# A second queue for row fetches: ScalarE takes over one gathered token of 26 tiles

## The chip, the core and the metric

The kernel runs on one core of a Trainium2 chip. The metric is device time in microseconds (us), from the kernel's start to its end. Engines are named as the profile names them: PE is TensorE (matmul), PEld its weight loads, DVE is VectorE, ACT is ScalarE, POOL is GpSimd, SP is SyncE. A name with a q (SPq) is an engine's queue, which issues transfers.

## The reference

A recommendation model for a batch of 16384 rows, in float32:

```
tok  = word_emb[token_idx].mean(axis=1)        # 32 tokens a row, table 50000 x 300
e1   = emb_mh1[mh1_idx].mean(axis=1)           # 20 indices a row, table 1000 x 64
e2, e3 likewise                                # tables 5000 x 64 and 10000 x 64
o1..o4 = emb_oh*[oh*_idx]                      # one index a row, small tables
emb  = concatenate([tok, e1, e2, e3, o1, o2, o3, o4], axis=1)     # 748 columns
wide = the sum of a scalar looked up for every small index
h    = relu(emb @ W1 + b1); h = relu(h @ W2 + b2); h = relu(h @ W3 + b3)   # 1024, 512, 256
out  = sigmoid(h @ Wd + bd + wide)
```

## The kernel before

The batch is cut into 128 tiles of 128 rows; a row of the batch is a partition. A tile goes through 11 steps, and the program's main loop runs over steps (1435 of them). One order for each engine is written out by hand: what the loop emits first stands first in each engine's queue, and an engine works its queue in order. Steps of different tiles overlap: counts of one tile, sums of the one before it, layers of earlier ones.

**Small tables.** They are not gathered. DVE makes one-hot rows by comparing an iota with the indices (`one_hots`, L402, tile `hot`), ACT scales a part of them (L409), PE multiplies them into counts (`counts`, L420, tile `pc`), ACT packs these into `cnt` (L423), and PE multiplies the counts of a whole tile with the tables kept on the chip (`small_sums`, L455, tile `pg`), which DVE adds up (L445). There are two buffers for `hot` and two for `pc`. The three layers run on PE at L578, and ACT evicts them at L589 into `h`.

**Tokens.** The 32 token rows of a tile are fetched from the 50000-row table in memory. POOL does most: one indirect DMA fetches the row of one token position for all 128 partitions, 1200 bytes each (L303, into `tok_rows`). Two positions make a group, a tile has 16 groups, and six buffers of two gathers each stand between POOL and DVE, which adds each gather onto the sum `own` (`add_up`: L279 for the first group, L281 and L286 after it). The adds follow the gathers by three groups (`TOK_LAG`) and are paced over the steps, so they stand in DVE's queue between the one-hots. The last add of a tile writes the features `g`.

**Rows by SyncE.** For two of three tiles (those from tile 4 with `t % 3` not 0, 83 in all) the last token position, 31, is not gathered. SP fetches it row by row (`fetch`, L347, into `fetched`): SP loads the position's 128 indices as a row (`load_column`, L320), DVE turns them into byte offsets with two small operations (`column_offsets`, L329 and L330), SP loads 32 of them at a time into registers (L338) and issues one transfer of 1200 bytes for each row. A fetch starts 25 or 19.5 steps ahead of the step by which the tile is summed, and its 128 rows are spread over 16.5 steps. Each transfer of a hardware queue takes the next of eight semaphores in turn, and waits until the transfer that had it before has landed.

SP also loads indices (`load_indices`, L357 and L361), weights and tables, and stores results (L631).

Of the kernel before, what the change touches and what calls it, by code (L numbers as in the profile page):

```python
# [31 lines left out]
COLUMN_AHEAD = 4  # L32
COLUMN_LAG = 1
LOADS = 32
ROW_BYTES = 4 * TOK_D
WAKE = 27
EARLY = 3
# [40 lines left out]
def kernel(  # L78
# [39 lines left out]
    ohp = ctx.enter_context(tc.tile_pool(name="onehot", bufs=HOT_BUFS))  # L118
    cp = ctx.enter_context(tc.tile_pool(name="counts", bufs=2))
    fp = ctx.enter_context(tc.tile_pool(name="fetched", bufs=2))  # L120
    gp = ctx.enter_context(tc.tile_pool(name="g", bufs=3))
    wp = ctx.enter_context(tc.tile_pool(name="wide", bufs=2))
    xp = ctx.enter_context(tc.tile_pool(name="x", bufs=1))
# [18 lines left out]
    chunk_at = [1, 1 + 2 * ROW, 1 + 4 * ROW, WIDE_AT, G_COLS - 2 * P, G_COLS - P]  # L142
    NK = len(chunk_rows)
    N_EARLY = 3

    ident = const.tile([P, P], F32, name="ident")
    make_identity(nc, ident)
# [22 lines left out]
    nc.vector.tensor_copy(own[:, 0 : n_h // 2], iota_s.bitcast(F32))  # L170
    iota = own[:, 0 : n_h // 2].bitcast(BF16)

    first = const.tile([P, 2, N_SMALL], I32, name="first")
    lookups = [("e1", N_MH), ("e2", N_MH), ("e3", N_MH), ("o1", 1), ("o2", 1), ("o3", 1), ("o4", 1)]
    at = 0
    for f, n in lookups:
# [1 line left out]
        at += n  # L178

    terms = const.tile([P, n_h, 3 * ROW], BF16, name="terms")  # L180
    minus_count = const.tile([P, P], BF16, name="minus_count")
    nc.vector.tensor_single_scalar(minus_count, ident, -1.0 / COUNT, op=ALU.mult)

    zeros = const.tile([P, ROW], F32, name="zeros")
    nc.vector.memset(zeros, 0.0)

    def load_tables(part0, tag):
        raw = hp.tile([P, PART, ROW], F32, name="raw", tag=tag)
        for f in SMALL:
            table, (h0, h1) = tables[f], slices[f]  # L190
            full, rest = divmod(table.shape[0], P)
            a, b = max(h0, part0), min(h0 + full, part0 + PART)
            if a < b:
                nc.sync.dma_start(
                    out=raw[:, a - part0 : b - part0, :],
                    in_=table[(a - h0) * P : (b - h0) * P, :].rearrange("(h p) d -> p h d", p=P),
                )
            if rest and part0 <= h0 + full < part0 + PART:
                nc.sync.dma_start(out=raw[rest:P, h0 + full - part0, :], in_=zeros[rest:P, :])
                nc.sync.dma_start(out=raw[0:rest, h0 + full - part0, :], in_=table[full * P :, :])  # L200
        return raw

    def convert_tables():
# [48 lines left out]
    def load_weights():  # L252

        nc.vector.memset(w1_sb[0:1, 3, :], 0.0)
        for k, rows in enumerate(chunk_rows):
            for at, a, b in rows:
                nc.sync.dma_start(out=w1_sb[at : at + b - a, k, :], in_=w1[a:b, :])
        nc.sync.dma_start(out=w2_sb, in_=w2.rearrange("(k p) m -> p k m", p=P))
        nc.sync.dma_start(out=w3_sb, in_=w3.rearrange("(k p) m -> p k m", p=P))
        for sb, dram in ((wd_sb, wd), (b1_sb, b1), (b2_sb, b2), (b3_sb, b3), (bd_sb, bd)):  # L260
            nc.sync.dma_start(out=sb, in_=dram)

    g_of = {}

    def features(t):
        if t not in g_of:
            g_of[t] = gp.tile([P, G_COLS], F32, name="g")
        return g_of[t]

    n_groups = N_TOK // TOK_GROUP  # L270
    n_all = B // P * n_groups + TOK_LAG
    summed = set()
# [15 lines left out]
    def tokens():  # L288

        under_way = []  # L290
        for n in range(n_all):
            if n < n_all - TOK_LAG:
                t, q = divmod(n, n_groups)
                it = token_indices[t // NSUB][:, t % NSUB, :].bitcast(U32)
                tok_rows = tokp.tile([P, TOK_GROUP * TOK_D], F32, name="tok_rows")
                rows = []
                for r in range(TOK_GROUP):
                    j = q * TOK_GROUP + r
                    if j == N_TOK - 1 and t in fetched:
                        rows.append(fetched.pop(t))  # L300
                        continue
                    rows.append(tok_rows[:, r * TOK_D : (r + 1) * TOK_D])
                    nc.gpsimd.indirect_dma_start(  # L303
                        out=rows[-1],
                        out_offset=None,
                        in_=word,
                        in_offset=bass.IndirectOffsetOnAxis(ap=it[:, j : j + 1], axis=0),
                    )
                under_way.append((t, q, rows))
            if n >= TOK_LAG:  # L310
                add_up(*under_way.pop(0))
            yield 1

    fetched, columns = {}, {}
    word_bytes = word.bitcast(U8).rearrange("n d -> (n d)").unsqueeze(0)

    def load_column(t):

        columns[t] = fp.tile([1, P], I32, name="column")
        nc.sync.dma_start(  # L320
            out=columns[t], in_=idx[t * P : (t + 1) * P, N_TOK - 1 : N_TOK].rearrange("n o -> o n")
        )

    def column_offsets(t):


        column = columns[t]
        low = ROW_BYTES & -ROW_BYTES
        nc.vector.tensor_single_scalar(column, column, ROW_BYTES // low, op=ALU.mult)  # L329
        nc.vector.tensor_single_scalar(column, column, low.bit_length() - 1, op=ALU.logical_shift_left)  # L330

    def fetch(t):


        rows = fp.tile([P, TOK_D], F32, name="fetched").bitcast(U8)
        column = columns.pop(t)
        for p0 in range(0, P, LOADS):
            _, values = nc.values_load_multi_w_load_instructions(  # L338
                column[:, p0 : p0 + LOADS],
                engines=[mybir.EngineType.SP],  # L340
                min_val=0,
                max_val=(word.shape[0] - 1) * ROW_BYTES,
                skip_runtime_bounds_check_because="the indices are rows of the table",
            )
            for i, value in enumerate(values):
                p = p0 + i
                nc.sync.dma_start(out=rows[p : p + 1, :], in_=word_bytes[:, bass.ds(value, ROW_BYTES)])  # L347
                if p == P - 1:
                    fetched[t] = rows.bitcast(F32)
                yield 1  # L350

    def load_indices(blk):


        b0 = blk * BLOCK
        it = idxp.tile([P, NSUB, N_TOK], I32, name="it")
        nc.sync.dma_start(  # L357
            out=it, in_=idx[b0 : b0 + BLOCK, 0:N_TOK].rearrange("(s p) c -> p s c", p=P)
        )
        ix = keyp.tile([P, 2, N_SMALL], I32, name="ix")  # L360
        nc.sync.dma_start(  # L361
            out=ix, in_=idx[b0 : b0 + BLOCK, IDX_MH:IDX_COLS].rearrange("(p f) c -> p f c", f=2)
        )
        token_indices[blk] = it
        return ix

    def lookup_keys(ix):
# [4 lines left out]
        keys = keyp.tile([P, 2, 2 * N_SMALL], BF16, name="keys", tag="keys")  # L372
        view = keys.rearrange("p w (f c) -> p w f c", f=2)
        nc.vector.tensor_copy(view[:, 0], low)
        nc.vector.tensor_add(view[:, 1], ix, first)
        return keys

    def key_columns(keys):
# [215 lines left out]
    def mlp(block, part=None):  # L594
# [19 lines left out]
        def finish():  # L614
# [13 lines left out]
            b0 = block.first * P  # L628

            def store():  # L630
                nc.sync.dma_start(out=out[b0 : b0 + n, :].rearrange("(a b) o -> o a b", b=P), in_=y)  # L631

            stores.append([STORE_LAG, store])

# [67 lines left out]
    fetches = [(summed_at(t) - FETCH_AHEAD[t % 3], t) for t in range(FETCH_FROM, tiles) if t % 3]  # L702
    fetching = []

    def speed(step):

        left = n_steps - step
        return 1 / (TILE_STEPS if left > WAKE else TILE_STEPS_SUMS if left > STEPS + EARLY else TILE_STEPS_LAST)
# [11 lines left out]
            block_of.update({t + k: block for k in range(n)})  # L720
        return block_of[t]

    ctx.enter_context(tc.manual_schedule())
    ix = load_indices(0)
    toks = Paced(tokens())
    tables_on_chip = convert_tables()
# [6 lines left out]
    for step in range(n_steps):  # L733
# [10 lines left out]
        if t < tiles:  # L744
# [5 lines left out]
            if i < STEPS - 1:  # L750
                hot = one_hots(sc, s, i + 1)
            elif t + 1 < tiles:
                hot = one_hots(next_sc if s == NSUB - 1 else sc, (s + 1) % NSUB, 0)
            flush_outputs()
            counts(cnt, hot_now, i)
            tables_on_chip.to(TABLE_PACE * (step - 2))
            if t == 1 and i == STEPS - 1:
                load_weights()
        else:
            flush_outputs()  # L760
        if sums:
            run_sums(sums, early_sums.get(i, 0), step, step)
        outputs = list(rows_out)
# [8 lines left out]
                    completed = step  # L772
        if complete and layers is None and step > completed:
            layers, target = start(complete.pop(0)), 0
        for at, t_f in fetches:
            if step == int(at) - COLUMN_AHEAD:
                load_column(t_f)
            if step == int(at) - COLUMN_LAG:
                column_offsets(t_f)
            if step == int(at):  # L780
                fetching.append((at, Paced(fetch(t_f))))
        for at, rows in list(fetching):
            rows.to(P * (step + 1 - at) / FETCH_STEPS)
            if step + 1 - at >= FETCH_STEPS:
                rows.finish()
                fetching.remove((at, rows))
        toks.to(tokens_by(step + 1))
        if t < tiles and more and s == 1 and i == (5 if t > 1 else 9):
            next_sc, evict = key_columns(next_keys)
# [26 lines left out]
    while complete or layers:  # L816
        if layers:
            layers.finish()
        layers = Paced(mlp(complete.pop(0))) if complete else None
    for _, k, ks in waiting:  # L820
        block = block_for(k)
        block.transpose(k, ks)()
# [43 lines left out]
```

## Time and profile before

| | |
|---|---|
| median of 3 runs | 5055.15 us (5052.5 to 5058.55) |
| the profiled execution, its time | 5052.86 us |
| its span, first to last instruction | 5050.9 us |
| granted TensorE clock, mean | 0.992 |
| busy: PE, DVE, ACT, POOL | 4810.5, 3716.8, 2723.9, 3798.2 us |
| gathers of POOL | 4013 |
| rows fetched by SP | 10624 = 83 x 128 |
| DMA engines' mean busy share | 4 to 5 tenths after the start |

A row of the groups reads: line, engine, operation, tile written and tiles read, count; then busy time in us and mean ns of one; then the idle time of the engine before these instructions, and what ended most of it. A row of the waits reads: who waited, for what, us in total, how often, the longest. A row of the timeline reads: start, duration, engine, line, and in brackets the idle time before it. A row of one source line gives least, median and greatest duration in ns. A row of the windows gives the stretch, then for PE, PEld, DVE, ACT and POOL the busy us and the number of instructions, then the granted clock, the DMA share and GB/s.

### The profile page before, as it was taken

Reading aid. Unit: us, or ns where it says so; the run is one execution under the profiler, and the core shown is the slowest. Engines: PE = TensorE matmul, PEld = TensorE weight load, DVE = VectorE, ACT = ScalarE, POOL = GpSimd, SP = SyncE. Lnnn points to the kernel's source line nnn. Section 1 sums busy time; section 2 is a strip of 40 time slices with the busy share of each in tenths; the row PEclk is TensorE's granted clock in tenths of the full one; section 3 lists DMA queues with packets and bytes.
Section 4 is the critical chain, followed back from the end, with each engine's and each line's share of the span. In section 5 each row is a group of like instructions: output and inputs, shape, how many; then the busy total and the mean of one; then the engine's idle time right before and its main releaser. Section 6 shows DMA issues by size and latency. Waiting matters only on the chain.

```text
span 5050.9 us, 117299 instructions
## 1 busy us (share of the span) xinstructions
PE 4810.5 (95%) x36356; PEld 3711.0 (73%) x36356; DVE 3716.8 (74%) x6778; ACT 2723.9 (54%) x3658; POOL 3798.2 (75%) x4020
## 2 busy tenths in 40 slices
PE   6799999999999999999999999999999999999999
PEld 4677776776777677677677777667767888888898
DVE  6777777777777777777777777777777777777774
ACT  5555555555555555555555555555555555555552
POOL 7777777777777777777777777777777777777775
PEclk9899999999999999999999999999999999999999
DMA  7444444444444444444444444444444444444443
GB/s 203 127 129 129 128 128 128 128 129 128 128 128 129 128 129 128 129 129 128 129 128 128 129 129 128 128 128 128 129 129 128 129 129 128 129 128 129 129 127 100
DMA packets 282526, 653.64 MB, mean 129 GB/s; under 512 B 140443, under 2 KB 151707, under 8 KB 281895
## 3 DMA queue, kind: packets, MB, share of 16 engines
q0 software_dynamic: 192624, 616.65, 45.3%
q1 hardware_dynamic: 89271, 29.49, 2.8%
q8 instruction: 284, 4.65, 0.4%
q14 instruction: 347, 2.84, 0.2%
HBM read 645.64 MB, written 0.07 MB: 128 GB/s over the span
## 4 chain that ended last, share of the span: by engine, by line
DMA 34%; DVE 19%; PE 17%; issue 16%; POOL 11%; ACT 2%; SPq 0%; DVEq 0%; POOLq 0%; ACTq 0%
DMA tok_rows<-in_word_emb_dram,it 34%; POOL tok_rows L303 11%; PE ph L578 8%; DVE hot L402 7%; DVE own L286 6%; PE pg L455 6%; DVE own L281 3%; PE pc L420 2%; DVE g L445 1%; ACT hot L409 1%; DVE own L279 0%; ACT cnt L423 0%; PE pc L496 0%; PE po L620 0%; SPq L347 0%
## 5 line engine op out<-in xcount | busy, mean ns | idle before, releaser
L303 POOL DMA_INDIRECT tok_rows<-in_word_emb_dram,it x4013 | 3797.3, 946 | 1225.2 <-issue 709.0
L409 ACT ACTIVATE hot<-hot 64x768 bf16<-64x768 bf16 (+1 forms) x1408 | 1155.4, 821 | 2065.3 <-DVE hot L402 2053.6
L455 PE MATMUL pg<-terms,cnt 128*128 128x195 bf16 x17664 | 1720.8, 249 | 57.2 <-DVE g L445 56.7
L455 PEld LDWEIGHTS <-cnt 128*128 128x128 fp8e3 x17664 | 1527.9, 98 | 105.7 <-issue 77.0
L578 PE MATMUL ph<-x,w_sb 128*128 128x384 f32 (+5 forms) x4932 | 1474.5, 436 | 21.1 <-ACT h L589 14.9
L402 DVE TENSOR_TENSOR hot<-own,sc 128x1656 bf16<-128x1656 bf16 (+1 forms) x1408 | 1394.1, 990 | 104.1 <-PE pc L420 12.5
L286 DVE TENSOR_TENSOR own<-own,tok_rows 128x300 f32<-128x300 f32 x1792 | 857.4, 478 | 593.9 <-DMA tok_rows<-in_word_emb_dram,it 551.5
L578 PE MATMUL ph<-h,w_sb 128*128 128x384 f32 (+2 forms) x4160 | 1225.6, 434 | 14.7 <-ACT h L589 14.6
L423 ACT ACTIVATE cnt<-pc 128x828 uint16<-128x828 f32 (+1 forms) x1408 | 1186.2, 842 | 68.8 <-PE pc L420 47.7
L281 DVE TENSOR_TENSOR own<-own,tok_rows 128x300 f32<-128x300 f32 x1920 | 917.7, 478 | 380.9 <-DMA tok_rows<-in_word_emb_dram,it 330.9
L578 PEld LDWEIGHTS ph<-x,w_sb 128*128 128x128 f32 (+1 forms) x4932 | 829.3, 191 | 313.9 <-ACT h L589 27.5
L420 PEld LDWEIGHTS <-hot 128*128 128x128 bf16 x8192 | 589.3, 98 | 531.1 <-issue 216.4
L578 PEld LDWEIGHTS ph<-h,w_sb 128*128 128x128 f32 x4160 | 698.8, 191 | 268.4 <-ACT h L589 29.7
L420 PE MATMUL pc<-hot 128*128 128x138 bf16 x8192 | 732.9, 224 | 109.6 <-ACT hot L409 81.0
L589 ACT ACTIVATE h<-ph,b_sb 128x384 f32<-128x384 f32 (+2 forms) x723 | 378.6, 524 | 123.9 <-PE ph L578 108.6
L445 DVE TENSOR_REDUCE g<-pg 128x130 f32<-128x390 f32 (+1 forms) x512 | 258.6, 505 | 68.4 <-PE pg L455 66.6
L500 DVE TENSOR_TENSOR x<-pc,scale 128x768 f32<-128x768 f32 x127 | 120.7, 950 | 43.8 <-PE pc L496 43.6
L496 PE MATMUL pc<-ident,g 128*128 128x128 f32 x762 | 107.0, 277 | 9.2 <-ACT cnt L423 7.9
L279 DVE TENSOR_TENSOR own<-tok_rows 128x300 f32<-128x300 f32 x128 | 61.4, 480 | 70.0 <-DMA tok_rows<-in_word_emb_dram,it 67.6
L496 PEld LDWEIGHTS pc<-ident,g 128*128 128x128 f32 x762 | 83.2, 142 | 14.7 <-ACT cnt L423 13.1
L620 PE MATMUL po<-h,wd_sb 128*1 128x384 f32 (+2 forms) x208 | 66.0, 438 | 2.0 <-ACT h L589 2.0
L627 ACT ACTIVATE x<-po,bd_sb 1x384 f32<-1x384 f32 (+2 forms) x52 | 26.7, 514 | 54.3 <-PE po L620 54.1
(57 smaller groups left out, 471.5 us busy)
## 6 DMA issues: line engine op xcount, KB each, us to landing
fetched<-in_word_emb_dram SPq DMA_DIRECT2D x10624, 1.2 KB
tok_rows<-in_word_emb_dram,it POOLq DMA_INDIRECT x4013
ix<-in_idx_dram SPq DMA_DIRECT2D x64, 64.0 KB
w_sb<-in_W_dram SPq DMA_DIRECT2D x6, 512.0 KB
raw<-in_mh_dram SPq DMA_DIRECT2D x4, 682.5 KB
it<-in_idx_dram SPq DMA_DIRECT2D x64, 32.0 KB
w_sb<-in_W_dram SPq DMA_DIRECT2D x1, 2048.0 KB
column<-in_idx_dram SPq DMA_DIRECT2D x83, 0.5 KB
```

Of the source, the lines that this page charges most:

```text
L281: nc.vector.tensor_add(tok_sum, tok_sum, a)
L286: nc.vector.tensor_add(to, tok_sum, b)
L303: nc.gpsimd.indirect_dma_start(out=rows[-1], out_offset=None, in_=word, in_offset=bass.IndirectOffsetOnAxis(ap=it[:, j : j + 1], axis=0),)
L402: nc.vector.tensor_tensor(hot[:, 0 : 2 * rows, :].rearrange("p i (n d) -> p i n d", d=2), iota.rearrange("p (n d) -> p n d", d=2).unsqueez ...
L409: nc.scalar.activation(upper, upper, AF.Copy, scale=UPPER)
L420: nc.tensor.matmul(pc[:, k // n, at : at + n_h], hot[:, 2 * k, 0:P], hot[:, 2 * k + 1, :], start=True, stop=True)
L423: nc.scalar.activation(cnt[:, :, b : b + rows].rearrange("l h (g k) -> l h g k", g=2), pc[:, :, 0 : n * n_h].rearrange("l g (k h) -> l h g ...
L445: nc.vector.tensor_reduce(field_columns(features(t), pair), pg[:, 0:n, :].rearrange("p f (c d) -> p f d c", c=3), AX.X, ALU.add,)
L455: nc.tensor.matmul(pg[:, j, :], by_slice[:, h, :], terms[:, h, :], start=(h == h0), stop=(h == h1 - 1))
L496: nc.tensor.transpose(pt[:, j // n, j % n, :], g[:, c : c + P], ident)
L578: nc.tensor.matmul(to, weights[: src.shape[0], k, m * P : (m + 1) * P], src, start=(k == 0), stop=(k == len(srcs) - 1),)
L589: nc.scalar.activation(dst()[:, m, 0:n], ph[:, 0:n], AF.Relu, bias=bias[:, m : m + 1])
```

## The change

Token position 30 of 26 tiles (from about tile 12 on) is no longer gathered by POOL. ACT fetches it row by row, with a queue of its own, into new buffers `fetched_scalar`: it loads the column of indices, DVE makes offsets of it, ACT loads 8 offsets at a time into registers and issues a transfer for each row. A helper `sync_dma` stands ahead of each of SP's transfers: when the next of the eight semaphores would be the seventh or eighth (`SCALAR_LANES`), ACT issues first, so that two rows of ACT follow six transfers of SP. A column for ACT is chosen when half the rows of the one before are out; the tile chosen is the first that is summed late enough at 2.55 rows a step and 5 steps of margin.

Rows of SP are now emitted in two portions in each step, before and after `counts`, where they were emitted in one portion later in the step. In `add_up` a row that is fetched comes first in its group. Two constants move into one of the new buffers, the columns share one tile, `first` is half as large, and POOL's order is kept by tokens in place of the written-out order.

The diff, cut to its core:

```diff
+LANES = 8
+SCALAR_LANES = (6, 7)
+SCALAR_FROM = 12
+SCALAR_RATE = 2.55
+SCALAR_MARGIN = 5.0
+SCALAR_LOADS = 8
+SCALAR_WANTED, SCALAR_LEAST = 8, 2
...
+    fa = ctx.enter_context(tc.tile_pool(name="fetched_scalar", bufs=2))
...
+    def hardware_dma(queue, **operands):
+        dma = queue.dma_start(**operands)
+        if transfers and transfers[-1][0] is not queue:
+            tc.add_manual_dep(
...
+        transfers.append((queue, dma.ins.name))
+
+    def sync_dma(**operands):
+        while len(transfers) % LANES in SCALAR_LANES and scalar_row and scalar_row[0]():
+            pass
+        hardware_dma(nc.sync, **operands)
...
-                    if j == N_TOK - 1 and t in fetched:
-                        rows.append(fetched.pop(t))
+                    if (t, j) in fetched:
+                        rows.insert(0, fetched.pop((t, j)))
                         continue
...
+        def choose(self, rows_before):
+            least = self.step + (rows_before + P) / SCALAR_RATE + SCALAR_MARGIN
+            t = next((t for t in range(tiles_all) if self.summed_at(t) >= least), None)
...
+        def load(self, free):
+            if len(self.values) >= (SCALAR_WANTED if free else SCALAR_LEAST):
+                return
...
+            self.values += load_offsets(self.column, self.loaded, SCALAR_LOADS, mybir.EngineType.Activation)
+            self.loaded += SCALAR_LOADS
+
+        def __call__(self):
...
+            value = self.values.pop(0)
+            p = self.row
+            hardware_dma(nc.scalar, out=self.rows[p : p + 1, :], in_=word_bytes[:, bass.ds(value, ROW_BYTES)])
+            self.row += 1
...
+    def fetch_rows(step, part):
...
+        for at, rows in list(fetching):
+            rows.to(P * (step + part - at) / FETCH_STEPS)
...
+        if scalar_row:
+            scalar.load(scalar.issued == issued)
...
+            fetch_rows(step, 0.5)
             flush_outputs()
             counts(cnt, hot_now, i)
+            fetch_rows(step, 1)
...
-        for at, rows in list(fetching):
-            rows.to(P * (step + 1 - at) / FETCH_STEPS)
```

## The prediction

> **What bounds the kernel now.** I read the page's busy table first, then the costliest groups, then the waits, then the timeline.
>
> ```profile
> PE 4810.5 (95%) x36356; PEld 3711.0 (73%) x36356; DVE 3716.8 (74%) x6778; ACT 2723.9 (54%) x3658; POOL 3798.2 (75%) x4020
> L303 POOL DMA_INDIRECT tok_rows<-in_word_emb_dram,it x4013 | 3797.3, 946 | 1225.2 <-issue 709.0
> ```
>
> The shares point at TensorE (PE) and would have us pass over POOL, but the POOL row must be read with its idle time: (3797.3 + 1225.2) / 4013 = 1.2515 us for each gather, and 4013 of them are 5022.5 us of a span of 5050.9. The timeline of POOL shows a metronome:
>
> ```profile
> 2000.12 0.94 POOL L303 DMA_INDIRECT tok_rows<-in_word_emb_dram,it  x1 [0.30 <-issue]
> 2001.37 0.94 POOL L303 DMA_INDIRECT tok_rows<-in_word_emb_dram,it  x1 [0.30 <-issue]
> 2002.62 0.95 POOL L303 DMA_INDIRECT tok_rows<-in_word_emb_dram,it  x1 [0.31 <-issue]
> ```
>
> Every gap is 0.30 us, whatever releaser is named beside it. From the records of all gathers, only 16 of 4012 start more than 1.3 us after the one before, 3 us of excess in all. So POOL never waits for a buffer: VectorE (DVE) always frees one in time, and it is DVE that waits for gathers.
>
> ```profile
> DVE own L286 <- DMA tok_rows<-in_word_emb_dram,it: 551.5, 853, 3.1
> DVE own L281 <- DMA tok_rows<-in_word_emb_dram,it: 330.9, 455, 2.9
> DVE hot L402 <- PE pc L420: 12.5, 19, 1.4
> ACT hot L409 <- DVE hot L402: 2053.6, 1272, 5.4
> ```
>
> DVE waits some 900 us for gathers and 12.5 us for PE's buffers; ACT (ScalarE) waits 2053.6 us for DVE. POOL sets the time; PE is close behind it.
>
> **The change, part by part.**
>
> *26 gathers leave POOL.* The changed order has 26 fewer gathers and nothing in their place: 26 x 1.2515 = 32.5 us. This lies wholly on the path.
>
> *Fetched rows are added first.* At the end of the last tile one add now runs before the last gather lands, where two follow it today:
>
> ```profile
> 5025.98 0.48 DVE L281 TENSOR_TENSOR own<-own,tok_rows 128x300 f32<-128x300 f32 x1 [0.72 <-DMA tok_rows<-in_word_emb_dram,it]
> 5026.49 0.47 DVE L286 TENSOR_TENSOR g<-own,fetched 128x300 f32<-128x300 f32 x1
> ```
>
> That saves 0.5 us. Elsewhere the adds keep their number and places. DVE gets 26 x (0.204 + 0.215) = 11 us of column arithmetic (durations of the same two operations at L329 and L330), beneath its 900 us of waiting.
>
> *ScalarE's queue.* In the changed order ACT's activations stand exactly as before. Between them come 3328 row transfers, 26 column loads and 416 register loads of 8 values. For a row the nearest rows are SyncE's (SP's):
>
> ```profile
> L347 SPq MOVE fetched<-in_word_emb_dram x10624: 29/29/39, 114.9 to 4996.0; - x197
> L347 SPq DMA_DIRECT2D fetched<-in_word_emb_dram x10624: 217/225/395, 115.0 to 4996.0; - x197
> L338 SPq TENSOR_LOAD <-column x332: 2026/2127/2360, 112.8 to 4983.6; - x166
> ```
>
> Undisturbed, SP starts a row every 0.32 us (the median of the starts). So ACT's sequencer gets 3354 x 0.32 = 1073 us. A load of 32 values takes 2.13 us; 8 values take between 0.53 (in proportion) and 2.13 us. The Trainium skill speaks against the lower end: "DMA: Bandwidth & Descriptors", section "Latency and other measured facts", gives such a load a floor of about 0.6 us. A line from 0.6 at one value to 2.13 at 32 gives an estimate of 0.94 for 8. By proportion the 416 loads are 220 us, by the page's floor 391, at the most 886. I take 391.
>
> Is it hidden? ACT's own work is 2723.9 us. Over the 1276 steps from tile 12 on (a step is 3.48 us between two `counts`) the addition is 1.15 us a step, against 1.46 of waiting for `hot` (2053.6 / 1408). It hides better than that, because ACT's sequencer runs ahead of its engine: its semaphore event for L627 at 770.500 lies inside the activation of 770.49 to 771.33. A pair of rows placed behind `hot` (0.84 us) or `cnt` (0.84) can thus be issued while that one runs.
>
> What doesn't hide is the wait on the two semaphores: a pair waits until the pair before has landed. In the trace's semaphore records a row of SP's lands 1.79 us after its start (median; 1.43 and 2.10 at the 5th and 95th per cent). A bad step: `hot` at 0, pair behind it, `cnt` at 0.84, second pair held to 1.8 and done at 2.5; the next `hot` is due at 3.5. With a load the sequencer is free at 3.4. So it fits, barely, and what stands behind it when it doesn't is `hot`, and PE behind `hot`: by the records PE starts `counts` 0.95 us (median; 0.35 at the lower quartile) after `hot` ends. Laying the changed ACT order over the trace's own ready times, `hot` comes about 0.05 us later on average. I put it at 0 to 5 us, and take 1.
>
> *SyncE's queue.* SP keeps its rows, with six semaphores for eight. Six rows take 6 x 0.32 = 1.92 us; 25% of rows land later than that, by 0.032 us averaged over all rows. A fetch of 128 rows thus loses between 0 and 4.1 us; since a delayed row also delays those behind it, not all adds up, and I take 3. Moving the rows to two places of a step changes only the order on SP, which has no engine waiting but DVE. SP has room:
>
> ```profile
> SPq L338 <- DVE own L281: 179.6, 27, 10.3
> SPq L338 <- DVE own L286: 161.0, 25, 11.1
> SPq L338 <- DVE hot L402: 119.1, 15, 12.5
> ```
>
> With the four smaller rows of this kind SP waits 577.8 us before its 83 fetches, 7.0 us each, and by the records the last row lands at least 10.8 us before DVE adds it. A step 0.65% shorter takes 0.4 of the 7.0, the semaphores 3: 3.6 us remain, cost nothing.
>
> *Two queues at once.* No row of this trace has two engines issuing. The Trainium skill, "Perfetto Trace Analysis", section "DMA Instruction — HWDGE (DVE, Sync)", says that the block that generates descriptors is shared and locked for one issuer: that speaks against the change. By the rule at its worst each ACT row holds SP up for a whole issue, 0.225 us; at the least for the generation alone: the 128-element column load (557 ns at L320) against a row's 225 gives 2.6 ns for each element, so nearly nothing for one row. I take the low end, some 0.03 us, since that slope is the nearest measurement; 40 ACT rows to a fetch (3328 / 83) then cost 1.2 of the 3.6 us. By the other end see below.
>
> *PE.* It must do the same work in 32 us less.
>
> ```profile
> 3500.00:4500.00 1000.00, 972.35 (x7570) 802.75 (x7569) 751.73 (x1360) 551.80 (x748) 756.31 (x800) 1.00 0.48 128
> 4900.00:5000.00 100.00, 97.52 (x947) 94.82 (x947) 56.61 (x112) 34.78 (x70) 75.36 (x80) 1.00 0.47 126
> ```
>
> Between 500 and 4900 us PE idles 146 us (4400 less the busy time of those windows). About 28 of the 33 us fall there: it must go from 96.7 to 97.3% busy; the two stretches above are at 97.2 and 97.5. As part of its idle time is DVE held by gathers, I count 1 us lost.
>
> **Sum.** 5050.9 - 32.5 - 0.5 + 1 + 1 = 5019.9 us of span; the profiled execution took 5052.86, 2 us over its span, so 5021.9; the median of the runs is 2.3 above that execution: 5024 us, 0.6% less. A measurement of this kernel can tell about 0.2%, 10 us, from no change.
>
> **The rivals.**
>
> *SyncE falls behind (slower).* The lock above is real. SP's spare 6.6 us a fetch then goes to 40 ACT rows; once rows are spread out, the six semaphores cost only some 1.4 us a fetch, so the turn comes at (6.6 - 1.4) / 40 = 0.13 us for each ACT row. Past it every fetch ends later than the one before, and after the 10.8 us margin DVE stands at the add of the last group, with `hot` queued behind it and PE behind that. At 0.225 us: 40 x 0.225 + 0.8 - 6.6 = 3.2 a fetch, over 77 fetches 246, less 10.8 and the 33 gained: about +200, 5255 us. At 0.15: about +35, 5090. For it: SP's issue occupies 70% of its time. Against: the slope above. Chance 0.12, with the neighbouring case that ACT does not issue beneath an activation (then 1.15 us a step meet 1.46 of waiting, half of it in the wrong place; 50 to 150 us of PE stalls by the same overlay, 5070 to 5170), which the event at 770.500 speaks against: 0.10. Together 0.22 slower.
>
> *PE becomes the bound.* If half or more of its idle time is its own (waits for its own results: L445 to L455 and back show 67 and 57 us), the gain is cut to a third to two thirds: 5033 to 5045. For: 97% busy. Against: DVE's 900 us. Chance 0.10, of which 0.04 within 0.2%.
>
> *Nothing to measure.* The POOL time is won and handed to stalls of ACT or SP of the same size: 5045 to 5065, chance 0.06. That the gathers are not taken out is excluded by the order.
>
> *My forecast*, 5016 to 5033: chance 0.62. With the faster part of the PE case 0.68 faster, 0.10 the same, 0.22 slower. The range from 5016 reaches into the slower cases to 5085, so that about 0.16 lies above it and 0.04 below. The forecast's own range is 5016 to 5033.
>
> **What would show it.** Right: 3987 gathers still 1.25 us apart with no gap; PE's idle time down by about 30 us; ACT's wait for `hot` down, PE's wait for `hot` (81 us at L420) not up by more than 10; SP's wait before its loads down from 578 to about 200 to 350 us; an ACT row near 0.23 us, a load near 0.9. Wrong: POOL gaps over 1.3 us released by DVE, DVE waiting for `fetched`, SP rows over 0.37 us apart, or gathers no longer evenly spaced.

## The result, and the profile after

The changed kernel takes 5020.66 us (median; 5019.4 to 5021.1 over 4 runs), the kernel before 5054.3 in the same comparison: the ratio is 0.9932 with a 95% interval of 0.9915 to 0.9949, some 34 us or 0.7% faster. The profiled execution took 5021.06 us, with a span of 5019.3. Nine of the twelve experiments below were run on three chips on which the kernel before itself takes 7220 to 7240 us; each is compared with that. The other three, which come first, ran where it takes 5057 to 5058 us.

First the busy table of the changed kernel's page, the shares of the chain of work that ended last, and the row of gathers:

```profile
PE 4806.3 (96%) x36356; PEld 3721.3 (74%) x36356; DVE 3748.7 (75%) x6830; ACT 2726.5 (54%) x3658; POOL 3774.2 (75%) x3994
...
PE 37%; DMA 26%; DVE 15%; issue 12%; POOL 9%; ACT 1%; SPq 1%; ACTq 0%; DVEq 0%; POOLq 0%
...
L337 POOL DMA_INDIRECT tok_rows<-in_word_emb_dram,it x3987 | 3773.3, 946 | 1219.3 <-issue 754.1
```

(3773.3 + 1219.3) / 3987 = 1.2522 us for each gather, the pitch of before, and 26 fewer of them. POOL's timeline shows the same beat:

```profile
2001.83 0.95 POOL L337 DMA_INDIRECT tok_rows<-in_word_emb_dram,it  x1 [0.30 <-issue]
2003.08 0.95 POOL L337 DMA_INDIRECT tok_rows<-in_word_emb_dram,it  x1 [0.30 <-issue]
2004.33 0.94 POOL L337 DMA_INDIRECT tok_rows<-in_word_emb_dram,it  x1 [0.30 <-DVE own L319]
```

Then the waits (who, for what, us in total, times, longest):

```profile
ACT hot L508 <- DVE hot L501: 1664.0, 1089, 5.0
...
DVE own L319 <- DMA tok_rows<-in_word_emb_dram,it: 468.5, 683, 2.8
...
DVE own L314 <- DMA tok_rows<-in_word_emb_dram,it: 221.0, 333, 3.1
...
ACT hot L508 <- DMA fetched_scalar<-in_word_emb_dram: 95.1, 92, 3.0
...
ACT h L688 <- DMA fetched_scalar<-in_word_emb_dram: 62.9, 84, 1.7
...
PE pc L519 <- ACT hot L508: 51.7, 34, 4.0
...
ACT cnt L522 <- DMA fetched_scalar<-in_word_emb_dram: 49.8, 67, 1.6
...
DVE hot L501 <- PE pc L519: 37.7, 55, 2.1
```

DVE still waits some 690 us for gathers, 190 less than before. New are 208 us in which an activation of ACT stands behind a row that waits for the landing of an earlier one. They do not lengthen PE's wait for `hot`, which fell from 81 to 52 us. DVE waits for no row that SP fetched. Next come the rows of the two hardware queues, where one line now issues for both (least, median, greatest ns):

```profile
L161 SPq DMA_DIRECT2D fetched<-in_word_emb_dram x10624: 217/225/604, 114.3 to 4966.2; - x197
...
L161 ACTq DMA_DIRECT2D fetched_scalar<-in_word_emb_dram x3328: 213/214/746, 309.9 to 4790.8; - x196
```

```profile
L375 ACTq TENSOR_LOAD <-columns x416: 716/763/1013, 307.0 to 4770.6; - x139
```

Where ACT's rows went is best seen in its timeline:

```profile
2000.23 0.84 ACT L508 ACTIVATE hot<-hot 64x768 bf16<-64x768 bf16 x1 [2.19 <-DVE hot L501]
2000.31 0.77 ACTq L161 DMA_DIRECT2D fetched_scalar<-in_word_emb_dram  x2
2001.13 0.87 ACT L522 ACTIVATE cnt<-pc 128x828 uint16<-128x828 f32 x1
2002.23 0.77 ACTq L161 DMA_DIRECT2D fetched_scalar<-in_word_emb_dram  x2
2003.05 0.84 ACT L508 ACTIVATE hot<-hot 64x768 bf16<-64x768 bf16 x1 [1.05 <-DVE hot L501]
```

The first pair is issued while `hot` runs, and `cnt` starts 0.06 us after `hot` ends. The second waits until 2002.23, by when the first has landed (a row of ACT lands 1.94 us after its start, median of the records), and is done at 2003.00, just before the next `hot`. By the records of all of ACT's transfers and register loads, 945 of their 1154 us lie beneath a running activation.

### The profile page after: what moved, and what is told of

The parts are those of the page before. It is cut to its first block, busy times and chain, and to the rows that moved or that the text cites. A ratio compares the mean times of both kernels' runs of the same rounds, so it can differ in the third digit from the quotient of the medians.

```text
span 5019.3 us, 124363 instructions
## 1 busy us (share of the span) xinstructions
PE 4806.3 (96%) x36356; PEld 3721.3 (74%) x36356; DVE 3748.7 (75%) x6830; ACT 2726.5 (54%) x3658; POOL 3774.2 (75%) x3994
## 4 chain that ended last, share of the span: by engine, by line
PE 37%; DMA 26%; DVE 15%; issue 12%; POOL 9%; ACT 1%; SPq 1%; ACTq 0%; DVEq 0%; POOLq 0%
DMA tok_rows<-in_word_emb_dram,it 23%; PE ph L677 17%; PE pg L554 14%; POOL tok_rows L337 9%; DVE hot L501 5%; DVE own L319 4%; PE pc L519 4%; DVE own L314 3%; DMA fetched_scalar<-in_word_emb_dram 1%; DMA fetched<-in_word_emb_dram 1%; PE pc L595 1%; DVE g L544 1%; PE po L719 1%; SPq L161 1%; DVE x L599 0%
## 5 line engine op out<-in xcount | busy, mean ns | idle before, releaser
L337 POOL DMA_INDIRECT tok_rows<-in_word_emb_dram,it x3987 | 3773.3, 946 | 1219.3 <-issue 754.1
L319 DVE TENSOR_TENSOR own<-own,tok_rows 128x300 f32<-128x300 f32 x1792 | 857.1, 478 | 513.3 <-DMA tok_rows<-in_word_emb_dram,it 468.5
L314 DVE TENSOR_TENSOR own<-own,tok_rows 128x300 f32<-128x300 f32 x1827 | 873.8, 478 | 271.9 <-DMA tok_rows<-in_word_emb_dram,it 221.0
L488 DVE COPY sc<-pc 128x512 bf16<-128x512 bf16 x64 | 44.0, 688 | 40.5 <-PE pc L484 39.8
```

Of the source, the lines that this page charges most:

```text
L314: nc.vector.tensor_add(tok_sum, tok_sum, a)
L319: nc.vector.tensor_add(to, tok_sum, b)
L337: gather = nc.gpsimd.indirect_dma_start(out=rows[-1], out_offset=None, in_=word, in_offset=bass.IndirectOffsetOnAxis(ap=it[:, j : j + 1], ...
```

## The experiments

The theory: POOL's pitch times the number of gathers sets the time, so 26 gathers are the whole gain, and the second queue is hidden. The rivals: part of the gain comes from the other edits; the queue costs something that the gain covers up; or PE is so near that the gain is already cut.

**The gain without the queue.** In the kernel before, a gather of every fifth tile is left out, and nothing stands in for it:

```diff
+                    if j == N_TOK - 3 and t % 5 == 0:
+                        rows.append(rows[0])
+                        continue
```

> The kernel before, with 26 gathers left out and nothing in their place: in every fifth tile position 29 is not gathered, and the row of position 28 is added twice (the adds keep their number; the sum of these tiles is not that of the reference). So the gain without the second queue. Theory (POOL sets the time; ScalarE's rows cost nothing): 5054.3 - 32.5 = 5022 us, the same as the changed kernel's 5020.7 within 3 us. Rival (the second queue costs something that is covered): clearly below, 5015 us or less. Where the kernel before takes some 7240 us, because the queues stand: no difference, since POOL does not set the time there.

Measured: 5026.1 us against 5057.0, ratio 0.9937 (0.9923 to 0.995), 31 us. Its row of gathers:

```profile
L306 POOL DMA_INDIRECT tok_rows<-in_word_emb_dram,it x3987 | 3773.5, 946 | 1218.5 <-issue 712.1
```

The count is that of the changed kernel, busy and idle time agree within 1 us, and the gain is the same: 0.9937 here, 0.9932 there. The difference of the two, 0.0005, is well inside their intervals (together about 0.002, some 11 us). The two profiles, one of each kernel, tell it more closely: from POOL's first start to its last it took 4989.6 us here and 4990.2 with the second queue. So over POOL's stretch the second queue and the other edits together cost some 0.7 us, and what the changed kernel gains is what 26 gathers are worth.

The time itself is 5.4 us above the changed kernel's, where it was expected within 3. In the profiled execution the difference lies behind the last gather, in PE. The first row is this run's, the second the changed kernel's (the last three figures are the granted clock, the DMA share and GB/s):

```profile
5002.00:5008.00 6.00, 5.03 (x22) 4.71 (x22) 0.00 (x0) 1.47 (x4) 0.00 (x0) 0.50 0.00 0
...
5003.00:5016.00 13.00, 13.00 (x117) 12.86 (x116) 0.00 (x0) 3.31 (x9) 0.00 (x0) 1.00 0.00 1
```

At a granted clock of 0.50 for part of that time PE took 25.3 us for its last 161 matmuls, and the kernel before 19.5 for as many. These 6 us come after all gathers and rows have landed. Why the clock fell there is not shown, and whether the other runs of this kernel have it too is not known.

**How far PE is.** The changed kernel with one more gather left out in each of the 128 tiles; the same three lines as above, for every tile:

```diff
+                    if j == N_TOK - 3 and True:
```

> The changed kernel with one more gather left out in every tile (position 29 is not gathered, the row of position 28 is added twice; the sums are not the reference's), 3859 gathers. On a chip where the kernel before takes some 5055 us. Theory A (POOL sets the time as long as it has work): 5021 - 128 x 1.2515 = 4861 us. Theory B (PE is close behind): PE's 4806 us of work, its idle time at the start (some 75 us in the first 250) and at the end, and waits of its own stop the time at 4930 to 4990 us, and POOL then waits for DVE. Where the queues stand as in the first set: about 0.9% below the kernel before.

Measured: 4903.1 us against 5056.9, ratio 0.9699 (0.9683 to 0.9716). That is between the two theories and fits neither: it is 118 us under the changed kernel, where 128 gathers would be worth 160. Its busy table, its chain's shares by engine, two waits and a stretch of 1000 us (the busy us of PE, PEld, DVE, ACT and POOL in it):

```profile
PE 4769.8 (97%) x36356; PEld 3713.0 (76%) x36356; DVE 3767.0 (77%) x6830; ACT 2732.4 (56%) x3658; POOL 3654.5 (75%) x3866
...
PE 68%; DMA 13%; DVE 6%; SPq 6%; issue 4%; POOL 2%; ACT 1%; ACTq 0%; DVEq 0%; POOLq 0%
```

```profile
DVE g L547 <- PE pg L557: 331.7, 237, 4.8
...
DVE own L319 <- DMA tok_rows<-in_word_emb_dram,it: 89.3, 125, 3.2
```

```profile
500.00:1500.00 1000.00, 992.57 (x7327) 735.59 (x7325) 787.04 (x1426) 564.53 (x733) 756.38 (x800) 1.00 0.49 129
```

Here the bound has changed hands. DVE's wait for gathers at L319 is down to 89 us, and it waits 332 us for PE; the chain runs 68% through PE, which was 37% in the changed kernel. PE is 99% busy in the stretch, and from 500 to 4500 us it idles 42 us, where the changed kernel left it idle for 109: most of its idle time was DVE's waiting for gathers, passed on. SP is near too: DVE now waits 32 us for its rows, and the chain has 6% in SP's queue. That answers the rival "PE becomes the bound": at 26 gathers fewer it is not, and somewhere between 26 and 154 fewer it is. Where in between was not run.

**More rows for ScalarE.** Three of eight semaphores, and 45 tiles:

```diff
-SCALAR_LANES = (6, 7)
-SCALAR_RATE = 2.55
+SCALAR_LANES = (5, 6, 7)
+SCALAR_RATE = 4.5
```

> Three of eight semaphores for ScalarE, five for SP; 45 tiles by ScalarE, 3968 gathers. On a chip where the kernel before takes some 5055 us. Theory (SP has little room; five rows in flight, each landing 1.93 us after its start, give at best 0.386 us a row, some 0.40 with the scatter; a fetch takes 62.9 us where 58.8 are there): SP falls behind, 5200 to 5360 us, DVE waits for fetched and gathers have gaps. Rival (POOL still sets the time): 5056 - 45 x 1.2515 = 5000 us. Where the queues stand as in the first set: about 2.3% over the kernel before.

Measured: 5327.1 us against 5058.2, ratio 1.0529 (1.0511 to 1.0546), with 19 gathers less than the changed kernel. The time is the theory's, and so is the engine that falls behind; the place where it is felt is not. The shares of the chain by line, and the waits:

```profile
DMA fetched<-in_word_emb_dram 22%; PE ph L677 14%; DMA fetched_scalar<-in_word_emb_dram 11%; PE pg L554 10%; SPq L161 6%; SPq L375 4%; DMA tok_rows<-in_word_emb_dram,it 4%; DVE hot L501 3%; PE pc L519 3%; POOL tok_rows L337 2%; ACTq L161 2%
```

```profile
DVE g L544 <- PE pg L554: 550.7, 301, 9.9
...
ACT hot L508 <- DMA fetched_scalar<-in_word_emb_dram: 336.3, 323, 5.3
ACT h L688 <- DMA fetched_scalar<-in_word_emb_dram: 317.7, 311, 3.4
ACT cnt L522 <- DMA fetched_scalar<-in_word_emb_dram: 303.7, 313, 2.8
DVE hot L501 <- PE pc L519: 251.5, 227, 7.0
...
PE pc L519 <- ACT hot L508: 157.0, 97, 5.2
...
ACT hot L508 <- DMA fetched<-in_word_emb_dram: 109.5, 35, 7.7
```

SP's queue too, in its own waits:

```profile
SPq L161 <- DMA fetched<-in_word_emb_dram: 523.8, 1718, 0.8
```

SP waits 524 us for landings of its own rows, where it waited 132 with two semaphores (lanes) for ACT, and its wait before its loads, its time to spare, is down from 314 us to 157. By the records one fetch starts 62.3 us after another, where it was 58.6 with two lanes and 62.9 were expected. The difference over 82 fetches is 310 us, and the span grew by 311: SP sets the pace, and its landings are the largest share of the chain.

But DVE waits only 21 us for `fetched`; it was expected to stand there. It is ACT that stands. 297 us of its waits are for rows of SP: by the records 165 of ACT's rows take over a semaphore from a row of SP (3 with two lanes), and 143 of these start within 0.2 us of that row's landing. Another 958 us of activations stand behind ACT's own rows (208 with two lanes), as its groups of three follow each other before the first have landed. PE in turn waits for `hot` three times as long, and DVE for PE.

PE's busy time is 110 us longer, at a mean granted clock of 0.971 (0.990 with two lanes), but PE also idles 414 us, where it idled 213, so it is not the bound. The run changes two things at once, a semaphore less for SP and more rows for ACT; what each costs by itself was not run.

The same edit was run twice on the chips named at the top:

> Three of eight semaphores go to ScalarE (at 4.5 rows a step), five stay with SP: 45 tiles by ScalarE, 3968 gathers. Theory (SP has little room, and a row lands 1.93 us after its start in the changed kernel's trace): five rows in flight give at best 0.386 us a row, some 0.40 with the scatter; a fetch takes 128 x 0.40 + 8.5 for loads + 3.2 for other transfers = 62.9 us where 58.8 are there; SP falls behind by about 4 us a fetch and sets the time: 5200 to 5360 us, with DVE waiting for fetched and gaps between gathers. Rival (POOL still sets the time): 5054.3 - 45 x 1.2515 = 4998 us.

1.0224 (1.0201 to 1.0247) there, and again:

> Three of eight semaphores for ScalarE (4.5 rows a step), five for SP; 45 tiles by ScalarE, 3968 gathers. Theory (SP has little room; five rows in flight, each landing 1.93 us after its start, give at best 0.386 us a row, some 0.40 with the scatter; a fetch takes 62.9 us where 58.8 are there): SP falls behind, 5200 to 5360 us, DVE waits for fetched and gathers have gaps. Rival (POOL still sets the time): 5056 - 45 x 1.2515 = 5000 us.

1.0243 (1.022 to 1.0266).

**On the other chips.** There POOL does not set the time. In the kernel without ScalarE's rows PE's weight loads come like this at times:

```profile
2033.58 0.10 PEld L554 LDWEIGHTS <-cnt 128*128 128x128 fp8e3 x1 [0.23 <-issue]
2034.29 0.10 PEld L554 LDWEIGHTS <-cnt 128*128 128x128 fp8e3 x1 [0.62 <-issue]
2035.01 0.10 PEld L554 LDWEIGHTS <-cnt 128*128 128x128 fp8e3 x1 [0.62 <-issue]
```

```profile
L337 POOL DMA_INDIRECT tok_rows<-in_word_emb_dram,it x4013 | 3799.0, 947 | 3395.9 <-DVE own L319 2000.3
```

That is one instruction every 0.71 us, waiting for nothing that the profile shows. By the records 1219 of SP's 10624 register moves take about 0.69 us there, where every one takes 29 to 39 ns in the changed kernel above. ACT's moves do not show it (41 ns at the most in the run with unused rows below), nor do POOL's gathers, with a median pitch of 1.251 us. The mean granted clock is 0.876, and PE is busy for 5618 us in place of 4806. What share of the 2200 us more these things make up could not be read from the traces. POOL waits 2000 us for DVE, as the row of the groups says, where nearly all its gaps were 0.30 us before. So these runs answer another question: what the edits cost where POOL has time to spare. The times that their expectations name were meant for chips where POOL sets the time, and were not put to the test.

Without ScalarE's rows, all other edits in (the condition that starts them is never true), twice:

```diff
-        if step == scalar_first and not scalar_row:
+        if False:
```

> The changed kernel without any row of ScalarE: SP has all eight semaphores again, POOL makes 4013 gathers, and all other edits stay (SP's rows in two portions of a step, fetched rows added first, POOL's order by tokens). Theory (the 26 gathers are the whole gain): 5054 us, as before, within 3 us; gathers 1.25 us apart without gaps. Rival (the other edits bring part of the gain): between 5021 and 5045 us.

> No rows of ScalarE at all, 4013 gathers, all other edits in. Theory: as the kernel before, 5055 within 3 us. Rival (the two portions of a step, the order of adds or the order tokens bring part of the gain): 5025 to 5047 us.

Measured: 1.0011 (0.9996 to 1.0026) and 1.0006 (0.9992 to 1.002). The other edits are worth nothing there. That they are worth nothing where POOL sets the time was not run by itself, but by the run without the queue these edits and the queue together come to no more than 11 us in the times, and to 0.7 us in POOL's stretch.

With the rows fetched and not used, so that POOL gathers them too (`fetched` is not set for position 30), three times:

```diff
             if self.row == P:
-                fetched[self.t, N_TOK - 2] = self.rows.bitcast(F32)
+                pass
```

> ScalarE fetches its 26 x 128 rows as in the changed kernel, but they are not used: POOL gathers position 30 of these tiles too, 4013 gathers. So the whole cost of the second queue is paid and nothing is gained. Theory (the queue's work is hidden, since POOL sets the time): 5054 us within 4 us, ACT's wait for hot lower by some 390 us than in the kernel before, POOL without gaps. Rival (the queue costs PE or SP time that the gain covers up): 5060 us or more.

> The same kernel as e2 (ScalarE fetches its rows, POOL gathers all 4013 as well, the rows are not used), again, since in the first set the kernel before took 7240 us with TensorE's queue standing[...] and POOL was not what set the time. Where the kernel before takes some 5054 us: theory (the queue's work is hidden while POOL sets the time): 5054 within 4 us, gathers 1.25 us apart without gaps. Rival (it costs PE or SP time that the gain covers up): 5060 us or more. Where TensorE's queue stands again: about 1.9% over the kernel before, as in e2.

> ScalarE's 26 x 128 rows are fetched and not used, POOL makes all 4013 gathers: the whole cost of the second queue without its gain. Theory (hidden while POOL sets the time): as the kernel before, 5055 within 4 us, gathers 1.25 us apart without gaps. Rival (it costs PE or SP time that the gain covers up): 5062 us or more.

Measured: 1.0187 (1.0166 to 1.0207), 1.0179 (1.0147 to 1.0212) and 1.0175 (1.0153 to 1.0196). The 1.9% named for this case held. So on these chips, where POOL waits for DVE, the second queue costs 1.8%, some 130 us.

With half of the tiles (`choose` returns nothing after the thirteenth):

> ScalarE fetches for the first 13 tiles only and then stops; 4000 gathers. Theory (time follows the number of gathers at 1.2515 us): 5054.3 - 16.3 = 5038 us, gathers evenly spaced in both halves. Rival (a saturating gain, PE being the bound already with few gathers less): nearer to 5021 us, all the gain with half of the tiles.

Measured: 1.006 (1.0038 to 1.0082). And with 128 gathers less than the changed kernel:

> The changed kernel with one more gather left out in every tile: position 29 is not gathered, the row of position 28 is added twice (the sums are not the reference's), 3859 gathers. Theory A (POOL sets the time as long as it has work): 5021 - 128 x 1.2515 = 4861 us. Theory B (PE is close behind): PE's 4806 us of work and the idle time at the start (some 75 us in the first 250) and at the end, plus waits of its own, stop the time at 4930 to 4990 us, and POOL then waits for DVE.

Measured: 0.9907 (0.9884 to 0.9931). From rows unused on the same chip to this, 154 gathers fewer are worth 1.0175 - 0.9907 = 2.7%, or 0.017% each, against 0.025% (1.2515 / 5055) where POOL sets the time. If each is worth the same, the changed kernel itself would stand there at 1.0175 less 26 x 0.00017, about 1.3% slower than the kernel before: an estimate, it was not run there. The half dose agrees with it: 0.6% measured, half of 1.3.

## Why the prediction was right, point by point

- *26 gathers, 32.5 us.* Shown, by the pitch and by the run without the queue. From POOL's first start to its last it took 5020.1 us before and 4990.2 after: 29.9 us less. The missing 2.6 us are a few gaps, one of 2.4 us near the end (at 4929) by itself; the run without the queue has such a gap at the same place, so it comes with the fewer gathers and not with ScalarE.
- *Fetched rows first, 0.5 us.* From the last gather's end to the last add's start it is 2.11 us after and 2.49 before: 0.4 us. The whole stretch from the last gather's end to the end of the span is 1.6 us shorter. Another 0.83 us of it is the output of an earlier block (L618 and L620), which stood in the last tile's chain at 5029.2 before and no longer does.
- *ScalarE's queue hidden.* Right, and the main wait came out as drawn: a second pair held until the first has landed, done before the next `hot`. `hot` stands 95 us in all behind landings, 0.07 us a time, where 0.05 was expected. A row takes 0.214 us (0.225 expected). A load of 8 takes 0.763, between the proportion (0.53) and the 0.94 got from the floor that the Trainium skill states ("DMA: Bandwidth & Descriptors", section "Latency and other measured facts"). Two measured points, 0.763 for 8 and 2.127 for 32, give 0.057 for each value and 0.31 besides, which leaves 0.37 for one value where the page has 0.6; only 8 and 32 were measured.
- *SyncE.* SP's wait before its loads fell from 577.8 to 314 us, within the 200 to 350 named. Six semaphores cost it 132 us in waits for its own rows, 1.6 a fetch; 3 were counted. But by the records the last row of a fetch now lands as little as 3.1 us before DVE adds it, where it was 10.8.
- *The shared block.* Not to be seen in the time of an issue. By the records a row of ACT takes 218 ns on average when SP issues in the same moment and 218 when it does not (no activation running in either case); SP's row takes 231 beside one of ACT and 228 otherwise: 3 ns, where the prediction counted 30. The lock that it takes from the Trainium skill ("Perfetto Trace Analysis", section "DMA Instruction — HWDGE (DVE, Sync)") could by its estimate have cost up to 225. SP's rows start 0.323 us apart (0.320 before; 0.37 was the sign of being wrong). So the slower rival did not come at two lanes. At three SP did fall behind, but by its waits for landings (524 us) and not by a lock: a row of SP took 230 ns beside one of ACT and 228 otherwise. (The rival's case of 0.15 us comes by its own terms to (40 x 0.15 + 1.4 - 6.6) x 77 - 10.8 - 33 = 18 us, not to 35.)
- *PE.* Its idle time from 500 to 4900 us fell from 146 to 122 us, as its busy time rose from 96.7 to 97.2%. The prediction's sum allowed for this, and the run of 128 fewer shows that more was there.
- *The sum.* 5019.9 us of span were expected and 5019.3 measured, in part by luck: POOL lost 2.6 us where 2 us were put down to ACT and PE, and the tail gave 1.1 more than was counted.

What failed is outside the prediction. For 128 fewer gathers, theory B took PE's busy time for a fixed 4806 us, of which the run has 4770, and its own waits for larger than they are. For three lanes, the stall was expected at DVE and came at ACT.

## What to carry to other kernels

Read the engine whose pitch never changes, not the one with the highest share: PE at 95% was waiting for POOL at 75%, whose idle time was part of each instruction. Work taken off such an engine is worth its pitch until the next engine is reached, and a run with that work simply left out tells beforehand what it is worth and where the next limit is. Where POOL set the time, a second queue on a compute engine cost nothing that could be measured: most of its transfers ran under activations, and the first queue kept time to spare. With a semaphore more for ACT and one less for SP, SP fell behind, and the kernel took 5% longer. On chips where POOL had time to spare, the second queue cost 1.8%.

## What was not expected of the hardware

- Rows of both queues land later with two queues than with one: by the records 1.93 us (SP) and 1.94 (ACT) after their start, where SP's alone took 1.79. What delays them was not tested.
- Of ACT's rows issued while an activation runs, some one in eight takes 0.45 us in place of 0.21; with none running nearly all take 0.21.
- On three chips SP's queue and PE's at times issue an instruction only every 0.7 us, and the second queue then costs 1.8%. What holds these two, and by which wait the second queue costs there, stays open.
